# Seven-product matrix schemes: running sums kept in one PSUM bank with ScalarE copies, in place of VectorE additions, and a new written order

## The chip, the cores and the metric

One core of one Trainium2 chip runs the whole program. The metric is device time in microseconds (us). All data is float32.

## The reference, cut to what matters

128 graphs of 64 nodes with 512 features pass through four graph layers, each with a layer norm and a relu ahead of it and a residual around it.

```python
for layer in (L0, L1, L2, L3):                      # x: [128, 64, 512], adj: [128, 64, 64]
    h = maximum(layernorm(x), 0)
    x = x + layer(h, adj)

L0: H = adj != 0
    conv(v, W) = Dn * (H @ (Be * (H.T @ (v @ W.T))))      # Dn, Be: inverse degrees
    h1 = layernorm(relu(conv(h, W1) + b1)) * gamma + beta # 512 -> 1024
    out = conv(h1, W2) + b2 + h                           # 1024 -> 512
L1: s = h @ w @ a;  A = exp(leaky(8 * tanh((s_i + s_j) / 8))) * adj
    out = (A / rowsum(A) * rowsum(adj)) @ h @ w
L2: P = adj * exp((h Wq + bq) (h Wk + bk).T);  out = (P / rowsum(P)) @ (h Wv + bv)
L3: Tr = rownorm(adj * exp(leaky(sj + si + ab)))
    out = relu(h Wk0 + Tr h Wk1 + Tr Tr h Wk2 + biases)
```

## The kernel before, in words

**Tiling.** The 8192 rows are cut into 16 groups of 512 rows, a group being four tiles of 128 rows (two graphs each). Layers 0 and 1 of all 16 groups come first; their results go to memory (`xm`), and layers 2 and 3 of all groups follow.

**The scheme.** Every large weight product is done on 2x2 blocks with seven products in place of eight (a Strassen-Winograd scheme; `strassen`, L589, and `seven`, L568). Of two row tiles and a weight in four blocks it makes sums of blocks (L599 on VectorE, the weights' sums once at the start, L393 to L396), seven products on TensorE (L607, in layer 2 L845), and four results that are sums of products. The products 1, 6 and 7 are running sums: M1, M1+M6 and M1+M6+M7. Layer 0 runs the scheme twice for each half of a group (a product is two matmuls of 512 columns for W1, four of 256 for W2), layer 1 once (two of 256), layer 2 twice for a group (queries and values, four of 256 side by side in one bank), layer 3 once for a half (six of 256). In all there are 64 schemes that fill a bank of 512 columns and 96 that fill 256.

**Sums before.** Each of the products 1, 6, 7 and 5 has a PSUM bank of its own. ScalarE copies M1 to the buffer U (L575), VectorE adds the second (L577) and the third (L579), reading each from PSUM. The products 2, 3 and 4 accumulate in the banks of 1, 5 and 7. The results go out through an emit function: for each of the four, VectorE reads the bank and adds bias, scale or residual; for three of them another operation first adds the running sum (VectorE L625 in W1 of layer 0, GpSimd L635, L799, L865, L899, L987 elsewhere), and the result (0,0) has none.

**What sets the order.** The kernel writes down the order of all instructions itself. Each operation is recorded with an engine, a cost in us and a priority; `Graph.run` (L82) takes for each engine the operation that can start first by these costs, and among equals the one of lowest priority. Priorities come from the group (`PERIOD1`, `PERIOD2`), a stretch for each layer and a shift for each part of the program (`AT`, L281). Buffers are handed out in the same pass; U has two places for 512 columns and one for 256, the transient buffer `qT` two, PSUM eight banks. Where TensorE would stand idle over 0.5 us by these costs, filling matmuls of 128x128 on ones are put in (L1013). At run time nothing is rearranged: each engine takes its list in order, and waits on semaphores.

**Other steps named below.** L467 multiplies Wq by Wk once, from loads L327. L437 needs all of W2. L546 mixes rows by the graph matrix and ScalarE L548 copies the result. L555 and L557 are ScalarE copies of 1024 half-words around a DMA transpose, whose buffer `tmp` is shared with loads of weights that VectorE's L381 consumes. L705 is the first product with the graph matrix. L667, L948, L957 and L973 belong to layer 3's transition matrix and its use; L878 are the logits of layer 2 and L911 its weighted values.

```python
        mul[1](p1, True)
        act(n / 1200 + 0.17, lambda: nc.scalar.copy(at(0)(), p1.t[:, :n]), [p1], [(U, 0)])
        mul[6](p2, True)
        dve(c_v(n), lambda: nc.vector.tensor_add(at(1)(), p2.t[:, :n], at(0)()), [p2, (U, 0)], [(U, 1)])
        mul[7](p4, True)
        dve(c_v(n), lambda: nc.vector.tensor_add(at(2)(), p4.t[:, :n], at(1)()), [p4, (U, 1)], [(U, 2)])
```

Of the kernel before, what the change touches and what calls it, by code (L numbers as in the profile page):

```python
# [11 lines left out]
ALU = mybir.AluOpType  # L12
# [4 lines left out]
D = 512  # L17
# [150 lines left out]
def tile_adj_preln_d4(  # L168
# [6 lines left out]
    nc = tc.nc  # L175
# [37 lines left out]
    for two in TWO:  # L213
        both = work.tile([P, max(sum(size(shape) * n for _, shape, n in tags) for tags in two)], F32,
                         name="_".join(tag for tags in two for tag, _, _ in tags))
        for tags in two:
            at = 0
            for tag, shape, n in tags:
                for i in range(n):
                    v = both[:, at:at + size(shape)]  # L220
# [28 lines left out]


    def c_mm(n, count):
        return 2 * count * max(n * 2 / 2400 + 0.0025, 0.111)

    TR = 0.109

    def c_v(n, from_psum=False):
        return n / 960 + 0.155 + 0.05 * from_psum
# [4 lines left out]
    def dve(cost, fn, r, w):  # L262
        return G.op("DVE", cost, fn, r, w)

    def act(cost, fn, r, w):
        return G.op("ACT", cost, fn, r, w)
# [7 lines left out]
    def quad(b):  # L274
# [2 lines left out]
    FILL = 0.75  # L277


    STRETCH, PERIOD1, PERIOD2 = (2.11, 6.43, 4.5, 0.21), 79.8, 140.53  # L280
    AT = {  # L281
        "x0": -1458.56, "apart": 58.27, "w1": -1207.06, "b1": -1268.61, "w2": 312.2, "w": -214.25, "c1": 103.95,
        "l0": -1592.46, "c2": -560.69, "l1": 125.29, "c": 849.04, "g0": -1279.86, "g1": -1456.39, "g2": -589.08,
        "g3": -1259.16, "g": -1258.76, "bq": 321.93, "l3": 56.2, "wg": 1603.23, "w3": 387.13, "beg0": -72.8,
        "beg1": 73.58, "end00": 0.51, "end01": 19.09, "end11": -75.14, "new2": 31.64, "new3": 4.77, "end2": -39.58,
        "end3": -21.31, "load1": -108.19, "load2": 27.97, "m": 12.29, "h0": 9.53, "p0": 10.98, "z0": -29.14,
        "q0": 15.48, "y0": -518.61, "h1": -26.33, "p1": -22.59, "z1": -30.25, "q1": 4.48, "y1": -2.94, "s": -20.64,
        "t0": -25.67, "e0": -522.9, "t1": -42.32, "e1": -53.88, "hT": 8.77, "sh": 220.05, "lq": 8.14, "pt": -124.53,
        "v": 35.92, "pv": -915.5, "s3": 19.84, "tt": -865.12, "a0": 46.62, "b0": -371.48, "a1": 104.26, "b1_": 198.72,
    }  # L290

    def part(name):
# [272 lines left out]
                nc.tensor.matmul(p.t, lhsT(c), rhs(c), start=first and c == 0, stop=last and c == k - 1)  # L565
        pe(c_mm(512, k), mm, r if first else [*r, p], [p])

    def seven(mul, U, n, emit):  # L568

        p1, p2, p3, p4 = (Buf("ps") for _ in range(4))
        at = lambda i: (lambda: U.t[:, i, :n])
        mul[1](p1, True)
        act(n / 1200 + 0.17, lambda: nc.scalar.copy(at(0)(), p1.t[:, :n]), [p1], [(U, 0)])  # L575
        mul[6](p2, True)
        dve(c_v(n), lambda: nc.vector.tensor_add(at(1)(), p2.t[:, :n], at(0)()), [p2, (U, 0)], [(U, 1)])  # L577
        mul[7](p4, True)
        dve(c_v(n), lambda: nc.vector.tensor_add(at(2)(), p4.t[:, :n], at(1)()), [p4, (U, 1)], [(U, 2)])  # L579
        mul[2](p1, False)  # L580
        emit(0, 0, p1, None, (U, 0))
        mul[5](p3, True)
        emit(1, 1, p3, (U, 2), (U, 2))
        mul[4](p4, False)
        emit(1, 0, p4, (U, 1), (U, 0))
        mul[3](p3, False)
        emit(0, 1, p3, (U, 1), (U, 1))

    def strassen(A, keys, B, kc, n, stag, emit):  # L589

# [30 lines left out]
    def scaled(dst, wdst, scale, ks, add, ka, p, u, v, n):  # L621

        if u is not None:
            (U, i), j, add0 = u, v[1], add
            dve(c_v(n) + 0.2, lambda: nc.vector.scalar_tensor_tensor(U.t[:, j], U.t[:, i], scale(), add0(), op0=ALU.mult, op1=ALU.add), [u, *ks, *ka], [v])  # L625
            add, ka = (lambda: U.t[:, j]), [v]
        dve(c_v(n, True), lambda: nc.vector.scalar_tensor_tensor(dst(), p.t[:, :n], scale(), add(), op0=ALU.mult, op1=ALU.add), [p, *ks, *ka], [wdst])  # L627

    def biased(dst, j, p, u, v, row, krow):

        cols = slice(j * D // 2, (j + 1) * D // 2)
        add, ka = (lambda: row()[:, cols]), krow
        if u is not None:
            (U, iu), iv = u, v[1]
            pool(0.75, lambda: nc.gpsimd.tensor_add(U.t[:, iv], U.t[:, iu], row()[:, cols]), [u, krow], [v])  # L635
            add, ka = (lambda: U.t[:, iv]), v
        dve(c_v(D // 2, True), lambda: nc.vector.tensor_add(dst.t[:, cols], p.t[:, :D // 2], add()), [p, ka], [(dst, j)])

    def across(col, r):

# [122 lines left out]
    def layer1(g):  # L763
        ad = adjs[g]
        sg = Buf("col")
        part("s")

        stats = [pre_stats(g, t) for t in range(T)]
        for t in range(T):
            h = pre_ln(g, t, stats[t])  # L770
            dot(lambda h=h: h.t, lambda: wa_b.t, lambda t=t: sg.t[:, t:t + 1], [h, wa_b], [(sg, t)])
        z = bcast_sum(lambda: sg.t, lambda: sg.t, [(sg, t) for t in range(T)])
        act(0.42, lambda: nc.scalar.activation(z.t, z.t, AF.Tanh, scale=0.125), [z], [z])
        lrelu(z, 0.1)
        act(0.42, lambda: nc.scalar.activation(z.t, z.t, AF.Exp, scale=8.0), [z], [z])


        PT, zz, den, num = Buf("bd"), Buf("ee"), Buf("col"), Buf("col")
        dve(0.42, lambda: nc.vector.tensor_reduce(num.t, ad.t[:, 0], AX.X, ALU.add), [ad], [num])
        dve(0.42, lambda: nc.vector.tensor_mul(zz.t, z.t, ad.t[:, 0]), [z, ad], [zz])  # L780
        dve(0.42, lambda: nc.vector.tensor_reduce(den.t, zz.t, AX.X, ALU.add), [zz], [den])
        dve(0.16, lambda: nc.vector.reciprocal(den.t, den.t), [den], [den])
        dve(0.16, lambda: nc.vector.tensor_mul(den.t, den.t, num.t), [den, num], [den])
        rn = across(lambda: den.t, [den])
        dve(0.42, lambda: nc.vector.tensor_mul(z.t, z.t, ad.t[:, 1]), [ad, zz], [z])
        for s in HALVES:
            dve(0.61, lambda s=s: nc.vector.tensor_mul(PT.t[s, :, s], z.t[s], by_node(rn, s)), [z, rn], [(PT, s.start)])
        PTk = [(PT, 0), (PT, C)]
        step(1.0)
        for t0 in (0, 2):  # L790
            part(f"t{t0 // 2}")
            ph = [left_mul_T(pre_ln(g, t, stats[t]), lambda t=t: PT.t[:, t, :], PTk, "mT") for t in (t0, t0 + 1)]
            step(1.8)

            def emit_w(i, j, p, u, v, t0=t0):
                xx, cols = xt[g, t0 + i], slice(j * D // 2, (j + 1) * D // 2)
                if u is not None:
                    U, iu = u
                    pool(0.75, lambda: nc.gpsimd.tensor_add(xx.t[:, cols], xx.t[:, cols], U.t[:, iu]), [xx, u], [xx])  # L799
                dve(c_v(D // 2), lambda: nc.vector.tensor_add(xx.t[:, cols], p.t[:, :D // 2], xx.t[:, cols]), [p, xx], [xx])  # L800

            part(f"e{t0 // 2}")
            strassen(lambda i, j, ph=ph: ph[i].t[:, 2 * j:2 * j + 2, :], {(i, j): [ph[i]] for i in range(2) for j in range(2)},
                     W, 2, D // 2, "s1", emit_w)
            for t in (t0, t0 + 1):
                xx = xt[g, t]
                xmid[g, t] = dram.tile([P, D], F32, name=f"xm{g}_{t}")
                dma(256, lambda xx=xx, t=t: nc.sync.dma_start(xmid[g, t], xx.t), [xx], [("xmid", g, t)])

    def layer2(g):  # L810
# [44 lines left out]
        def emit_q(i, j, p, u, v):  # L855
            if u is None:
                q = Buf("qT")
                for o in range(2):
                    act(0.38, lambda o=o: nc.scalar.activation(q.t[:, o, :], pair(p.t)[:, o, :], AF.Identity, bias=gb_c[:, 2 * i + o:2 * i + o + 1]), [p, "gb"], [(q, o)])
                qs.append((i, j, lambda: q.t, [(q, 0), (q, 1)]))  # L860
            else:

                (U, iu), iv = u, v[1]
                at = lambda: pair(U.t[:, iv])
                pool(1.3, lambda: nc.gpsimd.tensor_add(at(), pair(U.t[:, iu]), gb_c[:, 2 * i:2 * i + 2, None].to_broadcast([P, 2, 2 * P])), [u, "gb"], [v])  # L865
                dve(c_v(D), lambda: nc.vector.tensor_add(at(), pair(p.t), at()), [p], [v])
                qs.append((i, j, at, [v]))

        seven({n: prod(WG[n], hs[n], True) for n in range(1, 8)}, Buf("u5"), D, emit_q)


        def logits():
# [20 lines left out]
        def emit_v(i, j, p, u, v):  # L893
# [3 lines left out]
            if u is not None:  # L897
                (U, iu), iv = u, v[1]
                pool(1.3, lambda: nc.gpsimd.tensor_add(pair(U.t[:, iv]), pair(U.t[:, iu]), bias), [u, "bv_b"], [v])  # L899
                add, ka = (lambda: pair(U.t[:, iv])), v  # L900
            dve(c_v(D), lambda: nc.vector.tensor_add(vb[i].t[:, :, at], pair(p.t), add()), [p, ka], [(vb[i], j)])


        hv = {**hs, 3: hs[4], 4: hs[3], 5: hs[7], 7: hs[5]}
# [16 lines left out]
    def layer3(g):  # L921
# [39 lines left out]
        for t0 in (0, 2):  # L961
# [21 lines left out]
            def emit_o(i, j, p, u, v, t0=t0):  # L983
# [4 lines left out]
                    add2, ka = (lambda: U.t[:, iv]), v  # L988
                else:
                    add2 = add  # L990
                dve(c_v(D // 2), lambda: nc.vector.tensor_add(U.t[:, iv], p.t[:, :D // 2], add2()), [p, ka], [v])
                dve(c_v(D // 2), lambda: nc.vector.scalar_tensor_tensor(xx.t[:, cols], U.t[:, iv], 0.0, xx.t[:, cols], op0=ALU.max, op1=ALU.add), [v, xx], [(xx, j)])
                if (i, j) in ((1, 0), (0, 1)):
                    r = (g * T + t0 + i) * P
# [135 lines left out]
```

## Time and profile before

| | |
|---|---|
| median of 3 runs | 2374.13 us (2373.94 to 2375.01) |
| the profiled execution, first to last instruction | 2373.3 us, 0.8 us under the median of the runs |
| TensorE (PE) busy | 2349.7 us, 99% |
| VectorE (DVE) busy | 1742.1 us, 73% |
| ScalarE (ACT) busy | 1268.7 us, 53% |
| GpSimd (POOL) busy | 958.7 us, 40% |
| TensorE passes | 12008 (a float32 matmul is two passes) |

PE counts overlapping passes, so its busy share says little of how much of the time is needed work; the distance between the starts of passes says more. The program has 6004 matmuls, 82 of them filling ones. Layers 0 and 1 last until about 1170 us, layers 2 and 3 from about 1310 us; between them the two overlap.

### The profile page before, as it was taken

What the parts mean: (1) busy time and instruction counts of PE and PEld (TensorE: products, weight loads), DVE (VectorE), ACT (ScalarE), POOL (GpSimd) and SP (SyncE); (2) the same over time, 40 slices, a digit from 0 to 9 for tenths busy, and PEclk for the clock granted to TensorE, in tenths of its full rate; (3) what the DMA queues carried; (4) which work ended last, traced back from release to release, by engine and by line L of the source; (5) the groups of instructions that cost most, each with busy time, mean ns of one, the idle gap of its engine ahead of it and who ended that gap; (6) DMA issues with size and microseconds to landing.
All of it is one profiled execution on the core that took longest, in us unless ns stands there. A gap on an engine that the chain in (4) does not pass through costs nothing.

```text
span 2373.3 us, 33860 instructions
## 1 busy us (share of the span) xinstructions
PE 2349.7 (99%) x12008; PEld 1867.5 (79%) x12008; DVE 1742.1 (73%) x3798; ACT 1268.7 (53%) x1746; POOL 958.7 (40%) x1514
## 2 busy tenths in 40 slices
PE   9999999999999999999999999999999999999999
PEld 4677677777677776677788888888888888888887
DVE  7888778788778788777868566666666766667764
ACT  4566656567565576565745445444445444454422
POOL 6244455544455444555443323333323333323330
PEclk9999999999999999999999999999999999999999
DMA  7333222333223333232532322213322223322211
GB/s 258 80 80 65 54 68 64 71 80 63 50 68 69 72 80 54 55 73 71 133 106 59 76 69 61 69 45 69 76 64 65 64 52 73 71 63 65 48 36 40
DMA packets 336922, 171.02 MB, mean 72 GB/s; under 512 B 284656, under 2 KB 290672, under 8 KB 336752
## 3 DMA queue, kind: packets, MB, share of 16 engines
q1 hardware_dynamic: 336752, 168.86, 29.5%
q8 instruction: 94, 1.54, 0.3%
q14 instruction: 76, 0.62, 0.1%
HBM read 66.99 MB, written 34.70 MB: 43 GB/s over the span
## 4 chain that ended last, share of the span: by engine, by line
PE 89%; DVE 5%; DMA 3%; ACT 1%; issue 1%; POOL 1%; SPq 1%; DVEq 0%; ACTq 0%
PE ps L607 61%; PE ps L845 14%; PE ps L546 4%; PE ps L911 2%; PE ps L758 2%; PE ps L973 2%; PE ps L878 1%; DMA x<-xm 1%; DVE st L516 1%; PE ps L957 0%; DMA rw<-row 0%; PE ps L705 0%; DVE tmp_mB_s L599 0%; DVE o L381 0%; PE ps L467 0%
## 5 line engine op out<-in xcount | busy, mean ns | idle before, releaser
L537 ACT ACTIVATE h<-x,nm,rs 128x512 f32<-128x512 f32 x384 | 300.2, 810 | 399.6 <-POOL nm L524 366.8
L607 PE MATMUL ps<-wb_mem,s_s_a 128*128 128x256 f32 x2184 | 512.0, 380 | 0.3
L607 PEld LDWEIGHTS ps<-wb_mem,s_s_a 128*128 128x128 f32 x2184 | 409.5, 190 | 74.0 <-issue 19.8
L518 POOL TENSOR_SCALAR rs<-mv 128x1 f32<-128x1 f32 x320 | 99.2, 310 | 493.0 <-DVE mv L517 477.5
L607 PE MATMUL ps<-wb_mem,tmp_mB_s 128*128 128x256 f32 x1152 | 262.4, 380 | 3.2 <-DVE tmp_mB_s L599 3.1
L607 PEld LDWEIGHTS ps<-wb_mem,tmp_mB_s 128*128 128x128 f32 x1152 | 218.1, 190 | 35.3 <-DVE tmp_mB_s L599 5.4
L607 PE MATMUL ps<-wb_mem,mT_a 128*128 128x256 f32 x1016 | 242.0, 380 | 0.0
L607 PE MATMUL ps<-wa_mem,mT_a 128*128 128x512 f32 x512 | 237.3, 595 | 3.9 <-ACT mT_a L548 3.9
L607 PE MATMUL ps<-wb_mem,rT_vu_tt 128*128 128x256 f32 x1024 | 238.2, 380 | 0.6 <-ACT rT_vu_tt L557 0.6
L607 PEld LDWEIGHTS ps<-wb_mem,rT_vu_tt 128*128 128x128 f32 x1024 | 192.8, 191 | 41.3 <-issue 12.5
L607 PEld LDWEIGHTS ps<-wb_mem,mT_a 128*128 128x128 f32 x1016 | 192.2, 190 | 31.8 <-issue 5.7
L516 DVE BATCH_NORM_STATS2 st<-x 128x6 f32<-128x512 f32 x256 | 173.6, 678 | 45.8 <-DMA x<-xm 40.6
L519 POOL TENSOR_TENSOR rs<-rs,mhalf 128x1 f32<-128x1 f32 x320 | 193.3, 604 | 26.4
L607 PEld LDWEIGHTS ps<-wa_mem,mT_a 128*128 128x128 f32 x512 | 97.1, 190 | 112.7 <-issue 102.4
L607 PE MATMUL ps<-wa_mem,s_s_a 128*128 128x512 f32 x384 | 180.7, 593 | 0.3 <-DVE z_hT L627 0.3
L987 POOL TENSOR_TENSOR u<-u,bk_b 128x256 f32<-128x256 f32 x96 | 76.4, 796 | 238.9 <-DVE u L579 170.2
L575 ACT COPY u<-ps 128x256 f32<-128x256 f32 (+1 forms) x160 | 72.7, 454 | 177.8 <-PE ps L845 105.1
L635 POOL TENSOR_TENSOR u<-u,row_sh 128x256 f32<-128x256 f32 x96 | 74.9, 789 | 228.1 <-DVE u L577 211.6
L733 ACT ACTIVATE z_hT<-z_hT 128x512 f32<-128x512 f32 x128 | 79.6, 627 | 157.8 <-DVE z_hT L627 157.8
L557 ACT COPY rT_vu_tt<-z_hT 128x1024 uint16<-128x1024 uint16 x128 | 147.1, 1159 | 13.7 <-DMA z_hT<-tmp_mB_s 13.3
L546 PEld LDWEIGHTS ps<-bd,h 128*128 128x128 f32 x1024 | 131.1, 192 | 26.6 <-issue 22.2
L524 POOL TENSOR_SCALAR nm<-mv,rs 128x1 f32<-128x1 f32 x320 | 138.5, 433 | 31.1
(174 smaller groups left out, 4336.0 us busy)
## 6 DMA issues: line engine op xcount, KB each, us to landing
x<-in_x_dram SPq DMA_DIRECT2D x64, 256.0 KB, 2.7
xm<-x SPq DMA_DIRECT2D x64, 256.0 KB, 2.1
x<-xm SPq DMA_DIRECT2D x64, 256.0 KB, 2.8
out_dram<-x SPq DMA_DIRECT2D x64, 256.0 KB, 2.0
adj<-in_adj_dram SPq DMA_DIRECT2D x32, 256.0 KB, 4.0
rw<-row SPq DMA_DIRECT2D x94, 64.0 KB, 2.8
wb_mem<-in_Wk_dram SPq DMA_DIRECT2D x6, 512.0 KB, 5.3
tmp_mB_s<-in_Wk_dram SPq DMA_DIRECT2D x8, 256.0 KB, 3.1
```

Source lines behind the costliest of these rows:

```text
L516: dve(0.69, lambda i=i: nc.vector.bn_stats(st.t[:, i, :], src(i)), [r[i]], [(st, i)])
L518: pool(0.32, lambda: nc.gpsimd.tensor_scalar_add(rs.t, mv.t[:, 1:2], EPS), [mv], [rs])
L519: pool(0.65, lambda: nc.gpsimd.tensor_tensor(rs.t, rs.t, mhalf, ALU.pow), [rs], [rs])
L524: pool(0.47, lambda: nc.gpsimd.tensor_scalar(nm.t, mv.t[:, 0:1], rs.t, -1.0, op0=ALU.mult, op1=ALU.mult), [mv, rs], [nm])
L537: act(0.82, lambda: nc.scalar.activation(h.t, xx.t, AF.Relu, bias=nm.t, scale=rs.t), [xx, nm, rs], [h])
L546: nc.tensor.matmul(quad(p)[:, c, :], h.t[:, c * P:(c + 1) * P], rhs(), start=True, stop=True)
L557: act(1.16, lambda: nc.scalar.copy(u16(dst()).rearrange("p c (k q) -> p c k q", q=2), u16(back()).rearrange("p (q c r) -> p c r q", q=2, c ...
L607: nc.tensor.matmul(p.t[:, :n], lhs()[:, c, :], rhs(c), start=first and c == 0, stop=c == kc - 1, skip_group_check=True)
L635: pool(0.75, lambda: nc.gpsimd.tensor_add(U.t[:, iv], U.t[:, iu], row()[:, cols]), [u, krow], [v])
L733: act(0.63, lambda: nc.scalar.activation(z.t[:, cols], z.t[:, cols], AF.Relu), [(z, j)], [(z, j)])
L845: nc.tensor.matmul(pair(p.t)[:, o, :], a, b, start=first and o == 0 and c == 0, stop=c == 1, skip_group_check=True)
L987: pool(0.88, lambda: nc.gpsimd.tensor_add(U.t[:, iv], U.t[:, u[1]], add()), [u, ka], [v])
```

## The change

`seven` uses three banks. Product 6 and then product 7 are accumulated onto product 1 in the same bank; ScalarE copies the bank to U after each (`snap`). Product 4 is accumulated last in that bank, and its result is read from the bank with no further sum. Product 2 has a bank of its own and takes M1 from U. Product 5 is copied by ScalarE as well (to U, or to a `qT` buffer for the queries of layer 2), so that product 3 can be accumulated onto it; the result (1,1) is made of the two copies. The order of the products is 1, 2, 6, 5, 7, 3, 4 in place of 1, 6, 7, 2, 5, 4, 3. The emit functions read either a bank or a copy (`pv`).

The planner's cost of a matmul changes, and so do all stretches, periods and shifts, and by them the order of every engine's list. The list has 89 filling matmuls: 13 among the first 80 rows of TensorE's list, 44 where the layers overlap, 30 in fifteen pairs spread over layers 2 and 3, and 2 near the end. The loads of Wq and Wk stand first in the list of DMAs, ahead of adj and x.

```diff
     def c_mm(n, count):
-        return 2 * count * max(n * 2 / 2400 + 0.0025, 0.111)
+        return 2 * count * max(n * 2 / 2400 + 0.0045, 0.1115)
...
-    STRETCH, PERIOD1, PERIOD2 = (2.11, 6.43, 4.5, 0.21), 79.8, 140.53
+    STRETCH, PERIOD1, PERIOD2 = (2.2224, 5.134, 0.2702, 0.07), 81.1, 134.563
     AT = {
-        "x0": -1458.56, "apart": 58.27, "w1": -1207.06, "b1": -1268.61, "w2": 312.2, "w": -214.25, "c1": 103.95,
...
+        "x0": -2840.94, "apart": 287.74, "w1": -513.31, "b1": -168.3, "w2": 243.98, "w": 957.54, "c1": 854.05, "l0":
...
-    def seven(mul, U, n, emit):
-        p1, p2, p3, p4 = (Buf("ps") for _ in range(4))
-        at = lambda i: (lambda: U.t[:, i, :n])
-        mul[1](p1, True)
-        act(n / 1200 + 0.17, lambda: nc.scalar.copy(at(0)(), p1.t[:, :n]), [p1], [(U, 0)])
-        mul[6](p2, True)
-        dve(c_v(n), lambda: nc.vector.tensor_add(at(1)(), p2.t[:, :n], at(0)()), [p2, (U, 0)], [(U, 1)])
-        mul[7](p4, True)
-        dve(c_v(n), lambda: nc.vector.tensor_add(at(2)(), p4.t[:, :n], at(1)()), [p4, (U, 1)], [(U, 2)])
-        mul[2](p1, False)
-        emit(0, 0, p1, None, (U, 0))
-        mul[5](p3, True)
-        emit(1, 1, p3, (U, 2), (U, 2))
-        mul[4](p4, False)
-        emit(1, 0, p4, (U, 1), (U, 0))
-        mul[3](p3, False)
-        emit(0, 1, p3, (U, 1), (U, 1))
+    def pv(p):
+        t = p[0].t[:, p[1]] if isinstance(p, tuple) else p.t
+        return t.rearrange("p a b -> p (a b)") if len(t.shape) == 3 else t
+
+    def seven(mul, U, n, emit, fifth=None):
+        px, py, pz = (Buf("ps") for _ in range(3))
+        fifth = fifth or (U, 0)
+
+        def snap(p, v):
+            act(n / 1200 + 0.17, lambda: nc.scalar.copy(pv(v)[:, :n], p.t[:, :n]), [p], [v])
+
+        mul[1](px, True)
+        snap(px, (U, 0))
+        mul[2](py, True)
+        emit(0, 0, py, (U, 0), (U, 0))
+        mul[6](px, False)
+        snap(px, (U, 1))
+        mul[5](pz, True)
+        snap(pz, fifth)
+        mul[7](px, False)
+        snap(px, (U, 2))
+        emit(1, 1, fifth, (U, 2), (U, 2))
+        mul[3](pz, False)
+        emit(0, 1, pz, (U, 1), (U, 1))
+        mul[4](px, False)
+        emit(1, 0, px, None, (U, 0))
...
-        seven({n: prod(WG[n], hs[n], True) for n in range(1, 8)}, Buf("u5"), D, emit_q)
+        seven({n: prod(WG[n], hs[n], True) for n in range(1, 8)}, Buf("u5"), D, emit_q, Buf("qT"))
```

## The prediction

> **What bounds the kernel now.** I read the page's shares first, then the table by stage, then the timeline around each place where TensorE stood.
>
> ```profile
> PE 2349.7 (99%) x12008; PEld 1867.5 (79%) x12008; DVE 1742.1 (73%) x3798; ACT 1268.7 (53%) x1746; POOL 958.7 (40%) x1514
> ```
>
> ```profile
> 0.00:100.00 100.00, 91.89 (x309) 51.67 (x310) 80.53 (x159) 46.25 (x68) 47.74 (x70) 0.97 0.63 194
> 100.00:1170.00 1070.00, 1068.87 (x4531) 776.54 (x4530) 857.16 (x1887) 674.72 (x932) 520.35 (x824) 1.00 0.30 69
> 1170.00:1310.00 140.00, 135.52 (x817) 117.76 (x816) 108.93 (x238) 69.59 (x95) 55.08 (x90) 0.99 0.37 91
> 1310.00:2317.00 1007.00, 1002.56 (x6063) 876.67 (x6061) 672.92 (x1469) 468.21 (x637) 330.98 (x524) 1.00 0.26 62
> 2317.00:2373.00 56.00, 50.84 (x296) 44.82 (x294) 22.54 (x48) 9.95 (x16) 4.57 (x7) 0.96 0.14 41
> ```
>
> The first is the page's line of shares. In the second view the columns are the stretch, its length, then busy time and count for PE, weight loads, DVE, ACT and POOL, then granted clock, DMA share and GB/s. TensorE is the bound in every stretch. DVE is 80% busy in the first two, ACT 63% in the second.
>
> Busy time counts overlapping passes, so I also summed distances between starts. Undisturbed, a pass of 256 columns starts 0.216 us after the last, one of 512 columns 0.429, one of 128 columns 0.112 (0.056 at L973), one of L878 0.033. With the program's counts, 7424 x 0.216 + 1080 x 0.429 + 1024 x 0.112 + 1024 x 0.056 + 1024 x 0.033 + 268 short ones x 0.11 = about 2302 us are needed passes, which the change leaves alone. The 82 filling matmuls take 82 x 0.224 = 18.4. The rest of 2373.3 is 52.8: 1.0 before the first pass, 4.0 after the last, and between passes, by the same sum for each stage, 14.8, 2.4, 9.0, 17.2 and 3.5. Nothing else is there to win: some 65 us.
>
> ```profile
> 70.53 3.24 PE L607 MATMUL ps<-wa_mem,mT_a 128*128 128x512 f32 x4 [3.89 <-ACT mT_a L548]
> ...
> 2320.45 3.96 PE L1013 MATMUL ps<-ones 128*128 128x128 f32 x34
> 2325.85 1.10 PE L957 MATMUL ps<-rT_vu_tt,bd 128*128 128x64 f32 x8 [1.44 <-DVE rT_vu_tt L948]
> 2326.79 0.66 PE L1013 MATMUL ps<-ones 128*128 128x128 f32 x4
> 2327.42 5.41 PE L973 MATMUL ps<-rT_vu_tt,h 64*128 64x128 f32 x64
> ```
>
> Two examples (start, length, what, and in brackets idle time and releaser). At 66.6 TensorE stops 3.9 us for a ScalarE copy. Behind it ScalarE waited 5.2 us with a copy L555 for a `tmp` buffer that VectorE had not yet read, VectorE being busy without a break with weight sums and L381. Near the end only filling matmuls stand between layer 3's last chain and its use; 64 passes then take 5.4 us where 64 x 0.056 = 3.6 are due.
>
> **What the Trainium skill says.** "TensorE: Matmul & The Clock Gate", Part 1: after an idle window of about 3.4 us the array runs at half clock, until it has been busy for another. The trace agrees: the clock is 0.5 for 3.4 us at 71 and at 2327 us, each costing 1.7 us more. "PSUM — Partial Sum Buffer", PSUM bank collisions: TensorE and a reader must not be in one bank at once, so product 6 waits for the copy of M1 to end; no lag on top is stated. The trace has 0.2 us from the last pass's successor to a ScalarE copy (PE at 1413.24, ACT at 1413.44), and 0.05 us from a copy's end to the waiting pass (below). The same page, Engine vs sequencer instructions: ScalarE, VectorE and GpSimd take their lists strictly in order, so a copy behind a waiting one waits too; the 5.2 us above show it. Prices are the trace's.
>
> **The change, part by part.**
>
> ```profile
> L577 DVE TENSOR_TENSOR u<-ps,u 128x512 f32<-128x512 f32 x64 | 43.5, 680 | 12.1 <-PE ps L607 6.2 <-PE ps L845 5.9
> L575 ACT COPY u<-ps 128x512 f32<-128x512 f32 x64 | 37.4, 584 | 113.9 <-PE ps L845 105.1 <-PE ps L607 8.8
> L575 ACT COPY u<-ps 128x256 f32<-128x256 f32 x96 | 35.3, 368 | 63.8 <-PE ps L607 44.6 <-issue 13.2 <-DVE mv L517 3.6
> ```
>
> *Engine work.* VectorE loses L577 and L579: 64 x (0.680 + 0.686) + 96 x (0.422 + 0.421) = 168 us, from 73% to 66%. ScalarE goes from one copy for each scheme to four: 192 x 0.584 + 288 x 0.368 = 218 us more, from 53% to 63%; between 100 and 1170 us, with 32 schemes of 512 and 64 of 256, 127 us more, from 63% to 75%. Neither becomes the bound. The emit work keeps its count; (1,1) is now read from SBUF, which costs VectorE 0.793 (L625, all SBUF) against 0.746 (L627, PSUM), so under 64 x 0.05 = 3 us off the path. Matmuls: seven more fills.
>
> *New waits.* Each of products 6, 7, 4 waits for a ScalarE copy of the bank that it writes, product 3 for the copy of product 5; queued behind on PE is everything. In the written order I took, for each scheme product, the TensorE work between the bank's last use and the next. Under 1 us it is 51 times (before 16), from 1.5 to 2 us 128 times (before 36). A copy of 256 columns needs 0.2 + 0.37 + 0.05 = 0.62 against 0.86 in the narrowest (layer 1), one of 512 needs 0.2 + 0.58 + 0.05 = 0.83 against 1.73. So they fit as long as ScalarE is free; in layer 1's narrow run its list has the copies next to each other. What happens when not:
>
> ```profile
> 1237.41 1.04 ACT L555 COPY o<-h 128x1024 uint16<-128x1024 uint16 x1
> 1238.36 0.57 ACT L575 COPY u<-ps 128x512 f32<-128x512 f32 x1
> ...
> 1238.98 1.99 PE L845 MATMUL ps<-z_hT,wa_mem 128*128 128x256 f32 x8 [0.32 <-ACT u L575]
> ```
>
> Here a copy stood behind L555, and the next product, 1.73 us later in the bank, came 0.48 us late by starts. Also, the copy of product 5 goes where M1 was: ScalarE waits for the emit of (0,0) to have read it, mostly on GpSimd (0.8 us), which has two products' time.
>
> *100 to 1170 us.* Before, 2.4 us are lost. Of 52 tight reuses before one was late, so of 179 some four will be, 2 us in all; I put the 2 here (bounds 0 and 8, a third of the 51 narrow ones late by 0.48).
>
> *Start.* By hand with the trace's DMA landings (one of 256 KB each 0.7 us): Wq and Wk first brings L467 from 10.1 to about 4.3 us, at half clock for a part of it; adj and x come about 1 us later, hidden behind those 16 matmuls. The first two W1 products and all of L467 end near 27.7 us, where before the same work ends at 30.6: -2.9 (bounds -4 and +1). L437 is then reached early, and the last load of W2, behind a weight load that needs a `tmp` buffer, lands near 40: +2.2 (0 to +4). Nine fills after that become two: 7 x 0.224 = -1.6. The stop at 66.6 costs 4.0 and 1.7 for the clock; five schemes by then relieve VectorE of up to 10 x 0.68 = 7 us, but I take only 3.5 of the 5.7, since ScalarE's list grows there. Sum -5.8 (-11 to +3).
>
> *Where the layers overlap.* 44 fills for 43, other work alone on PE: +0.2 (-5 to +5).
>
> *1310 to 2317 us.* The 30 fills cost 30 x 0.224 = +6.7: they are placed where the planner sees TensorE idle, before product 6 and the logits. Of the 17.2 lost, 10.1 lie before L607 and L911, that is behind VectorE's block sums and layer 2's emits (waits named: `tmp_mB_s` L599 and `ve` L914); VectorE drops by 71 us there, and I take half, -5. Late copies beyond those above +1. Sum +2.7 (-8 to +12).
>
> *End.* L667 is now followed by three products and so is L957, 6 x 2 x 0.216 x 3 = 7.8 us, where the chain from L667 to L957 took 8.0. 17 fills fewer are -3.8; of the 3.5 lost I leave 0.7, with no idle window and so no half clock. Sum -6.6 (-7.7 to 0). The last product's emit stays two VectorE steps and a store.
>
> Together 2.0 - 5.8 + 0.2 + 2.7 - 6.6 = -7.5, so 2365.8 in the profiled execution, and 2366.6 beside the median.
>
> **The rivals.**
>
> *The relief goes further* (2356): the stop at 66.6 goes whole, and VectorE's 10.1 us in layers 2 and 3 as well: start -8.5, then -3.4, end -6.6. For it: DVE is the busiest after PE. Against: many waits there are for chains, not for load.
>
> *Nothing changes* (2374): the ends win 12, and the fills with new ScalarE waits in the middle give it back. The list has those 30 fills; that is a plan for idle time where before there was none.
>
> *Slower* (2384): the running bank becomes a chain through ScalarE. The place is the 128 + 51 tight reuses, 127 more than before, most in layers 1 and 2; the price is one copy of 1.04 to 1.16 us ahead in ScalarE's list, 0.48 us as seen. L555 and L557 fill (134 + 132 + 147 + 73 + 50 + 24) / 2373 = 24% of ScalarE's time; if ScalarE's fuller list puts one ahead of every second tight copy, 90 x 0.48 = 43 us, and with 12 won at start and end and the fills in layers 2 and 3 covering some 20 of it, about +10. It decides from about 25 late ones, 12 us. Against it: of the 52 tight reuses before, matched to their passes, one alone was late.
>
> **How the numbers follow.** The forecast has 0.43 (its own range 2360 to 2373), the further relief 0.12, no change 0.20, slower 0.25. About 0.2% (4.7 us) is what a measurement of this kernel can tell from no change. Faster by over that is below 2369.4: 0.7 of the forecast and the first rival, 0.42; within it the rest of the forecast and nearly all of "nothing changes", 0.31; slower 0.27. The range from 2353 to 2386 takes in the rivals' values, and leaves out a larger relief and a larger chain.
>
> **What would show it.** Right: no wait over 2 us on PE between 50 and 100 us; L973 at the end near 3.6 us for 64 passes, and no fills of 17; DVE near 1575 and ACT near 1487 us busy; 100 to 1170 us losing under 5 us. Wrong: PE waiting for ScalarE's `u` copies by over 10 us in all, a half clock in layers 2 and 3, or a new stop before L437.

## The result, and the profile after

The changed kernel takes 2403.5 us (median, 2403.1 to 2406.2), the kernel before 2374.6 us beside it on the same chip (2373.9 to 2375.0). The ratio is 1.0123, with an interval from 1.0109 to 1.0137: slower by 29 us, where 7.5 us less were forecast. The profiled execution spans 2400.9 us, 27.6 more than that of before.

First the page's line of shares, then the table by stage (stretch, its length, busy time and count of PE, weight loads, DVE, ACT and POOL, granted clock, DMA share, GB/s). The border before the last stretch stands 28 us later than in the table of before, so that the last stretch holds about the same work.

```profile
PE 2357.4 (98%) x12022; PEld 1866.8 (78%) x12022; DVE 1636.8 (68%) x3478; ACT 1454.4 (61%) x2226; POOL 976.9 (41%) x1514
```

```profile
0.00:100.00 100.00, 90.19 (x283) 48.10 (x284) 81.64 (x147) 52.95 (x82) 50.12 (x66) 0.95 0.63 195
100.00:1170.00 1070.00, 1054.07 (x4424) 759.55 (x4423) 798.62 (x1669) 755.31 (x1169) 514.01 (x814) 1.00 0.29 65
1170.00:1310.00 140.00, 134.75 (x838) 116.80 (x838) 104.02 (x223) 86.11 (x132) 64.96 (x97) 1.00 0.39 103
1310.00:2345.00 1035.00, 1026.29 (x6193) 896.66 (x6192) 631.54 (x1402) 548.39 (x823) 341.98 (x530) 1.00 0.27 63
2345.00:2400.90 55.90, 52.07 (x291) 45.69 (x289) 21.01 (x40) 11.67 (x23) 5.79 (x8) 1.00 0.13 38
```

The work did move as planned: VectorE is down by 105 us and ScalarE up by 186. But in the second row TensorE gets through 107 passes fewer than before in the same 1070 us, at full clock. VectorE is 75% busy there and ScalarE 71%, so TensorE is not short of work because one of them is full: something makes it wait. I took the prediction's own sum for each stage again (time between starts of passes beyond their undisturbed spacing), with the filling matmuls, counted by the time at which they run, beside it at 0.224 us each:

| stage | lost before | lost after | fills | change | predicted |
|---|---|---|---|---|---|
| start, to 100 us | 14.8 | 18.8 | 17 to 11 | +2.7 | -5.8 |
| 100 to 1170 | 2.4 | 22.3 | 7 to 2 | +18.7 | +2.0 |
| overlap | 9.0 | 8.8 | 39 to 48 | +1.8 | +0.2 |
| 1310 to the end's chain | 17.2 | 23.0 | 0 to 28 | +12.1 | +2.7 |
| end | 3.5 | 0.4 | 19 to 0 | -7.4 | -6.6 |

The sum is +27.9, against 27.6 between the spans. Two thirds of it lie in layers 0 and 1. The list of TensorE's waits (waiting line, releaser, us in total, times, longest; waits under 0.15 us are not listed) names where:

```profile
PE ps L769 <- DVE y_qT L648: 12.9, 12, 1.6
PE ps L618 <- ACT u L582: 7.4, 16, 3.1
PE ps L922 <- DVE rT_vu_tt L912: 4.2, 8, 0.6
PE ps L968 <- DVE rT_vu_tt L959: 3.4, 7, 1.0
```

The second line is the rival chain through ScalarE, and it is the smaller one: 9.4 us in all with 2.0 at L856, of which 3.1 are one stop near the start. Counted by starts of passes, with the short waits, it is some 13 us. The first line is new. L769 is the last step of layer 0 (L758 before), which multiplies the graph matrix by y; L648 is the emit that writes y. Following it back in the timeline of one group (start, length, what, idle time and releaser):

```profile
435.34 0.39 SPq L339 DMA_DIRECT2D adj<-in_adj_dram  x1
...
437.32 0.21 DVE L518 BATCH_NORM_AGGREGATE mv<-st 128x2 f32<-128x12 f32 x1
...
439.78 0.42 DVE L790 TENSOR_REDUCE col<-adj 128x4 f32<-128x256 f32 x1 [2.25 <-DMA adj<-in_adj_dram]
440.12 0.42 DVE L648 TENSOR_TENSOR y_qT<-u 128x256 f32<-128x256 f32 x1
...
440.45 0.42 DVE L648 TENSOR_TENSOR y_qT<-ps,u 128x256 f32<-128x256 f32 x1
...
440.92 1.13 PE L769 MATMUL ps<-y_qT,bd 128*128 128x512 f32 x2 [1.12 <-DVE y_qT L648]
```

VectorE is free at 437.5 and stands 2.25 us with a row sum of the next group's adj (L790, needed only in layer 1), because the load that was issued at 435.34 lands 4.4 us later. The y emits are next in its list, and TensorE waits 1.12 us behind them. Over the whole program this row sum waits 33.3 us in 14 groups:

```profile
L790 DVE TENSOR_REDUCE col<-adj x16: 386/420/421, 6.4 to 1028.5; 128x4 f32<-128x256 f32 x16
its engine sat idle before it (us, times) until:
  DMA adj<-in_adj_dram: 33.3, 14
```

Before, the same instruction (L779) began 9 to 24 us after the issue, mostly 22, and the same view names no wait. The row sum reads adj alone, nothing of the seven products. It is the new written order that put it there.

**Theories.** Theory 1: most of the loss is the order, that is, the place of instructions in the engines' lists, first of all this row sum. Theory 2, the rival: TensorE is held by ScalarE's copies between products in one bank, and the row sum is beside the point.

### The profile page after: what moved, and what is told of

It is laid out like the page before. It is cut to its first block, busy times and chain, and to the rows that moved or that the text cites. A ratio compares the mean times of both kernels' runs of the same rounds, so it can differ in the third digit from the quotient of the medians.

```text
span 2400.9 us, 33897 instructions
## 1 busy us (share of the span) xinstructions
PE 2357.4 (98%) x12022; PEld 1866.8 (78%) x12022; DVE 1636.8 (68%) x3478; ACT 1454.4 (61%) x2226; POOL 976.9 (41%) x1514
## 4 chain that ended last, share of the span: by engine, by line
PE 76%; DVE 10%; DMA 6%; POOL 4%; ACT 2%; issue 1%; SPq 0%; DVEq 0%; ACTq 0%; POOLq 0%
PE ps L618 56%; PE ps L856 8%; PE ps L547 4%; DMA adj<-in_adj_dram 2%; PE ps L769 2%; PE ps L984 2%; PE ps L922 1%; DMA rw<-row 1%; POOL nm L525 1%; POOL rs L520 1%; POOL x L810 1%; DVE st L517 1%; DMA row<-col 1%; DVE x L928 1%; DVE rT_vu_tt L959 1%
## 5 line engine op out<-in xcount | busy, mean ns | idle before, releaser
L582 ACT COPY u<-ps 128x256 f32<-128x256 f32 (+1 forms) x624 | 274.7, 452 | 450.6 <-PE ps L618 279.0
L618 PE MATMUL ps<-wb_mem,s_s_a 128*128 128x256 f32 x2184 | 507.2, 380 | 3.4 <-ACT u L582 3.4
L618 PEld LDWEIGHTS ps<-wb_mem,s_s_a 128*128 128x128 f32 x2184 | 410.8, 190 | 68.2 <-issue 8.5
L519 POOL TENSOR_SCALAR rs<-mv 128x1 f32<-128x1 f32 x320 | 108.5, 339 | 458.6 <-DVE mv L518 443.4
L618 PE MATMUL ps<-wb_mem,tmp_mB_s 128*128 128x256 f32 x1152 | 259.8, 380 | 0.7 <-ACT u L582 0.7
L618 PE MATMUL ps<-wa_mem,mT_a 128*128 128x512 f32 x512 | 241.7, 600 | 3.3 <-ACT u L582 3.3
L618 PEld LDWEIGHTS ps<-wb_mem,tmp_mB_s 128*128 128x128 f32 x1152 | 218.1, 190 | 30.9 <-ACT u L582 1.5
L618 PE MATMUL ps<-wb_mem,rT_vu_tt 128*128 128x256 f32 x1024 | 241.2, 379 | 0.5 <-ACT rT_vu_tt L558 0.5
L618 PE MATMUL ps<-wb_mem,mT_a 128*128 128x256 f32 x1016 | 237.8, 379 | 0.0
L618 PEld LDWEIGHTS ps<-wb_mem,rT_vu_tt 128*128 128x128 f32 x1024 | 192.6, 190 | 53.1 <-issue 28.4
L520 POOL TENSOR_TENSOR rs<-rs,mhalf 128x1 f32<-128x1 f32 x320 | 209.4, 655 | 25.2
L618 PEld LDWEIGHTS ps<-wb_mem,mT_a 128*128 128x128 f32 x1016 | 192.3, 190 | 31.8 <-issue 6.2
L618 PE MATMUL ps<-wa_mem,s_s_a 128*128 128x512 f32 x384 | 178.2, 594 | 0.0
L618 PEld LDWEIGHTS ps<-wa_mem,mT_a 128*128 128x128 f32 x512 | 96.4, 192 | 100.9 <-issue 92.3
L525 POOL TENSOR_SCALAR nm<-mv,rs 128x1 f32<-128x1 f32 x320 | 146.3, 457 | 31.5
L547 PEld LDWEIGHTS ps<-bd,h 128*128 128x128 f32 x1024 | 131.7, 193 | 31.3 <-issue 13.2
L810 POOL TENSOR_TENSOR x<-x,u 128x256 f32<-128x256 f32 x96 | 76.7, 799 | 166.5 <-ACT u L582 166.5
L556 ACT COPY tmp_mB_s<-z_hT 128x1024 uint16<-128x1024 uint16 x128 | 133.7, 1045 | 10.1 <-DVE o L382 5.6
```

What stands on the lines that cost most here:

```text
L519: pool(0.32, lambda: nc.gpsimd.tensor_scalar_add(rs.t, mv.t[:, 1:2], EPS), [mv], [rs])
L520: pool(0.65, lambda: nc.gpsimd.tensor_tensor(rs.t, rs.t, mhalf, ALU.pow), [rs], [rs])
L525: pool(0.47, lambda: nc.gpsimd.tensor_scalar(nm.t, mv.t[:, 0:1], rs.t, -1.0, op0=ALU.mult, op1=ALU.mult), [mv, rs], [nm])
L547: nc.tensor.matmul(quad(p)[:, c, :], h.t[:, c * P:(c + 1) * P], rhs(), start=True, stop=True)
L556: act(1.05, lambda: nc.scalar.copy(u16(planes.t).rearrange("p (q c) -> p q c", q=2), u16(src()).rearrange("p (c q) -> p q c", q=2)), ksrc, ...
L582: act(n / 1200 + 0.17, lambda: nc.scalar.copy(pv(v)[:, :n], p.t[:, :n]), [p], [v])
```

## Experiments

**The row sum alone, moved late in the changed kernel.** All lists stay as they were, save that each L790 stands right ahead of the one instruction that uses it.

```diff
+        early = {o.tag[1]: (t, q, o) for t, q, o in order if o.tag and o.tag[0] == "num"}
+        order = [e for _, q, o in order if not (o.tag and o.tag[0] == "num")
+                 for e in ([early[o.tag[1]]] if o.tag else []) + [(_, q, o)]]
```

> The changed kernel, with one instruction for each group of layer 1 moved in VectorE's list: the row sum of the next adj (L790) stands right ahead of its only use, no longer ahead of the y emits (L648). All else of the order is as in the changed kernel. Theory 1 (the written order: this row sum waits for adj's load 33 us in all, the y emits behind it, and TensorE's L769 behind them): the 14.8 us that TensorE loses between L618 and L769 from 100 to 1170 us go nearly all, so 2388 to 2391 us, a gain of 12 to 15 us, and L769 waits under 3 us for y. Theory 2 (TensorE waits for ScalarE's copies between products in one bank): the row sum is not on the path, 2403 us within 2.

Measured 2385.0 us, 1.0052 of before (1.0035 to 1.0068) against 1.0123. By the ratios that is 17 us less, by the spans 18.6, and so somewhat more than the 12 to 15 expected. The loss from 100 to 1170 us falls from 22.3 to 6.6. In the list of waits for this kernel L773 is the old L769, and the lines above it are other steps:

```profile
PE ps L622 <- ACT u L586: 6.0, 17, 1.7
PE ps L926 <- DVE rT_vu_tt L916: 3.9, 8, 0.6
...
PE ps L773 <- DVE y_qT L652: 0.6, 1, 0.6
```

So one instruction of 0.42 us for each group, in the wrong place of a list, is some 60% of the loss (67% by the spans).

**The reverse: the row sum early in the kernel before.**

```diff
...
+        from_ = sorted((t + 2.7, o.tag[1]) for t, q, o in order if o.tag and o.tag[0] == "adj")
+        order = [e for e in order if not (e[2].tag and e[2].tag[0] == "num")]
+        order = sorted(order + [(t, -1, early[g][2]) for t, g in from_], key=lambda x: x[:2])
```

> The kernel before, with the row sum of each next adj (L779) moved forward in VectorE's list to about 2 us after adj's load was issued, so ahead of three of the four y emits, as the changed order has it; its result goes to a buffer of its own, and the seven products are those of before. Theory 1: VectorE waits some 2 us for adj in each group, TensorE loses about 1.2 us in each of 13 or so groups: 10 to 16 us more than before, 2384 to 2390 us. Theory 2: the place of this one instruction does not matter, 2374 us within 2.

Measured 2380.0 us, 1.0032 (1.0019 to 1.0045), 7.5 us more. The sign is right, the size was too high: in that list VectorE comes to the row sum later after the issue, so it waits 11.3 us in 14 groups and not 33, and the loss from 100 to 1170 us rises by 5.9. The old scheme pays for such a place as well.

**The planner's number behind it.** The planner lets a load of 256 KB land 2.7 us after its issue begins. In the trace of the changed kernel the loads of x, of that size, do so (2.7 us, median), but those of adj take 4.1. The kernel before was planned with the same 2.7; its numbers only happened to put the row sum later. Here only adj's landing is changed, and all is planned anew.

```diff
-        dma(256, lambda: nc.sync.dma_start(b.t, adj[g]), [], [b])
+        dma(256, lambda: nc.sync.dma_start(b.t, adj[g]), [], [b]).late = 1.8
...
-            end = t + o.cost + self.LATENCY[o.eng]
+            end = t + o.cost + self.LATENCY[o.eng] + o.late
```

> The changed kernel with one number of the planner put right: a load of adj lands 4.5 us after its issue begins, as the trace has it, where the planner reckoned 2.7. The whole order is planned anew by this; it has 103 filling matmuls for 89, which is 3 us more. Theory 1 (the loss from 100 to 1170 us is this one wrong landing time): VectorE waits for adj by under 10 us in all where it waited 33, the 15 us at L769 go, and with the fills 2388 to 2394 us. If the loss came from the scheme or the other numbers: 2403 to 2408 us.

Measured 2388.7 us, 1.0070 (1.0055 to 1.0085): some 13 us less than the change, with 14 fills more. The row sum's waits for adj fall by two thirds (to 11.7 us, where under 10 were expected), and the loss from 100 to 1170 us to 7.7:

```profile
L791 DVE TENSOR_REDUCE col<-adj x16: 366/420/422, 5.5 to 1015.7; 128x4 f32<-128x256 f32 x16
its engine sat idle before it (us, times) until:
  DMA adj<-in_adj_dram: 11.7, 13
```

**What the copies cost.** The order of the changed kernel, but ScalarE's copies move 32 columns (182 ns each in place of 371 and 581), except in layer 2's queries; the rest of those sums is left out of the results.

```diff
-            act(n / 1200 + 0.17, lambda: nc.scalar.copy(pv(v)[:, :n], p.t[:, :n]), [p], [v])
+            act(n / 1200 + 0.17, lambda: nc.scalar.copy(pv(v)[:, :m], p.t[:, :m]), [p], [v])
```

> The changed kernel at its own order, but ScalarE's copies of the running sums move 32 columns in place of 256 or 512, except in the queries of layer 2. The other columns of those sums are left out of the results; all else runs as before. It takes some 70% of the duration off 600 copies and so bounds what copies cost in time. Theory 2 (the chain through ScalarE is the loss): 15 to 28 us less, 2375 to 2388 us. Theory 1 (the order is the loss, the copies fit beside other work): under 5 us less, 2398 to 2403 us; TensorE's waits for copies were 9 us in all in the profile of the changed kernel, of which a part goes.

Measured 2394.0 us, 1.0090 (1.0075 to 1.0105), 8 us less. That is below what theory 2 asked for and above what I had given theory 1: copies of 32 columns win some 8 of the 29 us, with L769 still losing 12.0 us between passes. By stages the loss between passes falls by 1.4 us at the start, 5.0 from 100 to 1170 and 4.4 after 1310 us, and rises by 1.6 where the layers overlap. Not all of the 5.0 is the copies' doing: in the run without late fills (below), whose lists up to there are those of the changed kernel, L769 loses 12.2 us and the stage 2.9 less than in the changed kernel. So something that runs through the copies does cost time, but how much of it falls in this stage one trace can't say. The next two runs look for it.

**A shared place behind them.** With the row sum late, 4.2 us remained at the first product after a mixing, 0.38 us in each of 12 groups. The timeline of that kernel at one of them:

```profile
385.84 1.17 POOL L814 TENSOR_TENSOR x<-x,u 128x256 f32<-128x256 f32 x1
...
386.97 1.26 POOL L737 TENSOR_TENSOR x<-x,h 128x512 f32<-128x512 f32 x1
387.04 1.47 DVE L815 TENSOR_TENSOR x<-u,x 128x256 f32<-128x256 f32 x1 [0.62 <-POOL x L814]
...
388.55 0.37 ACT L586 COPY u<-ps 128x256 f32<-128x256 f32 x1 [1.81 <-DVE x L815]
...
388.97 0.91 PE L622 MATMUL ps<-wb_mem,s_s_a 128*128 128x256 f32 x3 [0.22 <-ACT u L586]
```

The result (1,1) is now read from U. Its add (L815) waits for GpSimd's L814, then lasts 1.47 us where 0.41 is usual, beside GpSimd's L737; the copy of the next scheme's M1 goes to the same place of U (there is one for 256 columns) and waits 1.81 us; product 6 accumulates in the bank being copied, and waits for that. The edit gives product 5's copy a buffer of its own:

```diff
-        fifth = fifth or (U, 0)
+        fifth = fifth or (Fifth if n == D // 2 else tuple)((U, 0))
...
-        t = p[0].t[:, p[1]] if isinstance(p, tuple) else p.t
+        t = fifth_t if isinstance(p, Fifth) else p[0].t[:, p[1]] if isinstance(p, tuple) else p.t
```

> The kernel with the late row sum (2385 us), and the copy of product 5 in the schemes of 256 columns goes to a buffer of its own, no longer to the place of M1; the order of all lists is the same. In the run before this one TensorE still lost 0.38 us in each of 12 groups at the first product after a mixing (4.2 us in all): ScalarE's copy of the next M1 waits there for VectorE to read product 5's copy from the same place. Theory 1 (the order, and beside it this shared place): these 4.2 us go, 2380 to 2382 us. Theory 2 (copies are late because ScalarE is full): the place does not matter, 2385 us within 2.

Measured 2382.0 us, 1.0042 (1.0028 to 1.0055). In the trace the stage loses 3.0 us where it lost 6.6, near the 4.2 expected; in the whole only 1.5 us (spans) to 2.9 us (medians) come out, which the intervals don't tell from none. The other stages lose about 2 us more. So from 100 to 1170 us the new scheme in the mended order loses as little as the old one (2.4).

**Short copies in the mended order.** The same cut to 32 columns as above, with the same columns left out.

> The kernel with the late row sum and product 5's copy apart (2382 us), with ScalarE's copies of the running sums cut to 32 columns, except in the queries of layer 2; the other columns are left out of the results. It asks how much of the 9 us that short copies won in the changed kernel was the same time as the two mends won. If copies as such still hold TensorE up: 9 us less again, 2373 us. If, as theory 1 has it, part of those 9 us was the stall at the shared place and the queue around the row sum: 4 to 5 us less, 2377 to 2378 us, most of it from 1310 us on.

Measured 2379.7 us, 1.0036 (1.0022 to 1.0051): 1.4 us less by the ratios, 3.7 by the spans, 2.9 of it from 1310 us on. Below both expectations by the ratios. From 100 to 1170 us short copies win nothing more (3.1 us lost for 3.0), so what they won there the two mends had won by then. With the fills in place and the queries' copies whole, the length of the copies costs TensorE some 1 to 4 us of 2400; the intervals of the two runs overlap.

**The fills in layers 2 and 3.**

```diff
-        for _ in range(int(gap * FILL / (0.224 if filled else 0.448))):
+        for _ in range(0 if 12 <= len(filled) < 27 else int(gap * FILL / (0.224 if filled else 0.448))):
```

> The changed kernel without the fifteen pairs of filling matmuls that are spread over layers 2 and 3. If they stand on the path for nothing, each costs its 0.224 us: 6.7 us less, 2396.7 us. If they only take up time in which TensorE would have waited anyway, no change, 2403 us within 1.5, and 6.7 us more of waits between passes from 1310 to 2317 us.

Measured 2400.6 us, 1.0120 (1.0105 to 1.0135): 0.7 us less by the ratios, which is no difference, and 3.9 less by the spans. The loss between passes in that stage rises by 4.2 us where 6.7 of fills went. So the fills mostly cover real waits, as their placing said; my +6.7 for them was rightly on the bill, but as waits. And they are mostly the waits of theory 2: the rise is at L856 (7.0 to 11.4 us between passes from 1310 us on), and over the whole program its passes that start late behind a copy to `u` go from 4, costing 2.6 us, to 14, costing 6.0. In every second group, where a pair of fills stood ahead of product 6 of the queries, product 7 now starts some 0.3 us late behind ScalarE's copy. Most of these waits are too short for the list, which has 2.0 us in 3 for the changed kernel and here:

```profile
PE ps L856 <- ACT u L582: 3.0, 5, 1.3
```

So in layer 2 the new scheme pays for its copies in part with fills. Both runs with short copies kept these fills and the full copies of the queries, so they don't see this part.

**Either half alone.** The old seven products with the new numbers, and the new ones with the old numbers.

> One half of the change alone: the seven products of the kernel before, with the changed costs, periods and shifts of the planner. The list has 369 filling matmuls for 82, 64 us more of them. If the numbers alone were the loss of 29 us and the scheme free, about 2403 us plus what of the 64 us is not cover: 2410 to 2470. If the scheme were the loss, it would stay near 2374 plus the same.

> The other half alone: the new seven products with the planner's numbers of the kernel before. The list has 551 filling matmuls, 105 us more than before, ten of them in each group of layer 0, where the planner sees the next scheme wait. The row sum of adj stands early here too. If numbers and scheme only fit each other, it is the slowest of the four, 2440 to 2500 us; if the changed numbers were the loss by themselves, it would be under 2400.

Measured 2465.1 us (1.0387, 1.0372 to 1.0403) and 2546.9 us (1.0732, 1.0714 to 1.0750). The first lies in the range for the numbers alone, which its fills make wide. It has 287 fills more, 64 us, and 28 us beyond them (22 by the spans); from 100 to 1170 us it loses 21.8 us with the old scheme, as much as the changed kernel, though mostly at L547 waiting for `bd`, and its row sum waits only 3 times. The second is 47 us above my range: 105 us of fills and 69 beyond, among them 22 us at L967, behind VectorE's transposes L958, and some 14 at L983. Numbers and scheme belong together, so this pair can't divide the loss between them; the edits at a fixed order do.

**All mends together.** Late row sum, product 5's copy apart, no fills in layers 2 and 3, and at the start two `tmp` copies behind the copies that TensorE waits for:

```diff
+        for k, n in ((0, 1), (1, 2)):
+            i = [i for i, (_, _, o) in enumerate(order) if o.tag == ("plane",)][k]
+            j = [j for j, (_, _, o) in enumerate(order) if j > i and o.eng == "ACT"][n - 1]
...
+            order[j:j] = move
```

> The kernel with the late row sum and product 5's copy apart, and two more edits of the order: the fifteen pairs of filling matmuls in layers 2 and 3 are left out (3 us by the run without them), and in the first 70 us two of ScalarE's copies ahead of a DMA transpose, each waiting for a tmp buffer, stand behind the one and the two copies that TensorE waits for. Theory 1: 2380 to 2382 less 3 for the fills and less 2 to 4 for the start, 2373 to 2377 us, so level with the kernel before. Theory 2 (a full ScalarE): 2380 us or more.

Measured 2379.6 us, 1.0032 (1.0021 to 1.0044). That is still slower than before, misses the 2373 to 2377 expected, and can't be told from the run without the last two edits (1.0028 to 1.0055). By the number alone it lies at the mark set for theory 2. By stages it loses 2.8 us from 100 to 1170 us, so there theory 1 holds; from 1310 us on it loses 26.9 where 17.2 were lost before, and 10.5 us of the whole are late starts behind copies to `u`, so there part of the rest is theory 2. The edit at the start failed: the stop only moved on, to L468 (L451 in the changed kernel), which waits 6.4 us in two stops for VectorE's L466.

## Why the prediction was wrong, step by step

**100 to 1170 us: the step that failed, +2 against +18.7.** "Before, 2.4 us are lost. Of 52 tight reuses before one was late, so of 179 some four will be, 2 us in all." I looked at the new order only for bank reuse, the thing that the scheme changes. The order of the other lists was new as well, and I did not compare VectorE's instructions that depend on a load with the place of that load in SP's list. Before, adj landed 4.0 us after its issue; in the new list VectorE is free for the row sum about 2 us after it, ahead of the y emits. Both were there to be read. In place of the 2 us for late copies came 14.8 us at L769, behind the row sum's 33.3 us of waiting; with the row sum moved the stage loses 6.6. The term for bank reuse itself was too small, but inside its bounds of 0 to 8: TensorE's listed waits for copies are 2.5 us in this stage and 4.3 by starts, and none of the 4.3 is left once product 5's copy has its own buffer. The prediction saw that shared place in one direction only: product 5's copy waiting until M1 is read, not the next M1 waiting until product 5's copy is read.

**Start: +2.7 against -5.8.** The stop at 66.6 us was to lose more than half of its 5.7. The timeline of the changed kernel there:

```profile
64.67 0.69 DVE L382 SCALAR_TENSOR_TENSOR o<-tmp_mB_s 128x512 f32<-128x512 f32 x1 [0.97 <-DMA tmp_mB_s<-in_Wv_dram]
...
65.45 1.04 ACT L556 COPY tmp_mB_s<-z_hT 128x1024 uint16<-128x1024 uint16 x1 [5.58 <-DVE o L382]
...
66.40 0.85 ACT L582 COPY u<-ps 128x512 f32<-128x512 f32 x2
...
67.03 3.78 PE L618 MATMUL ps<-wa_mem,mT_a 128*128 128x512 f32 x4 [3.08 <-ACT u L582]
```

It is the same stop: the `tmp` copy waits 5.6 us for the same work of VectorE, and the copies that TensorE needs stand behind it. VectorE in its turn waits 0.97 us here for a load of weights into such a buffer; how much of the 5.6 is VectorE's load and how much the buffers was not separated. The stop costs 3.1 us, and the four passes after it run at half clock (3.78 us), so about 5 where 5.7 were lost before and 2.2 forecast. The failed term is the 3.5 us of relief: VectorE's lighter load did not end this wait sooner. Other stops came in: by starts 1.9 us at L443, 1.4 at L618, 1.2 at L451 and 1.9 at L547. L468 (L467 before) does begin at 4.28 us, as forecast, but the first mixing then waits, so the first W1 products and all of L468 end at 30.0 us and not at 27.7.

**1310 to 2317 us: +12.1 against +2.7.** The fills came as priced (28 of them here, 6.3 us). The half of 10.1 us that I gave to VectorE's relief came at one place and was lost at others: the loss at L607 did shrink (5.9 to 1.9), but the new order has layer 3's chain and layer 2's values late on VectorE (L968, behind L959: 4.6 us; L922, mostly behind L912: 7.5 for 4.2). Neither goes away with the row sum or without the fills. Short copies take 3 us off L968 and none off L922. Which placing would cure them was not tried, so their cause stays open.

**Where the layers overlap: +1.8 against +0.2.** Right within its bounds. **End: -7.4 against -6.6.** Right, and for the reason given: no fills stand there, and 64 passes take 3.8 us at full clock.

```profile
2348.02 1.00 PE L968 MATMUL ps<-rT_vu_tt,bd 128*128 128x64 f32 x8
2348.86 2.81 PE L618 MATMUL ps<-wb_mem,mT_a 128*128 128x256 f32 x12
...
2356.78 3.84 PE L984 MATMUL ps<-rT_vu_tt,h 64*128 64x128 f32 x64
```

**Engine work.** ScalarE came to 1454 us (1487 expected), VectorE to 1637 (1574 expected). Some 25 of VectorE's 63 us too many are the result (1,1), "under 3 us off the path": the prediction priced it for the 64 schemes of 512 columns from an operation that read SBUF alone, and the time went into the adds of 256 columns, see below. Some 28 more are older operations with inputs in SBUF alone (L610, L382, L636), which last longer in the new order; why was not looked into. Of the rivals, the slower one had the sign right, but mainly by another mechanism: late copies cost some 13 us by starts and part of what the fills cover, not 43.

## What to carry to other kernels

When an edit comes with a new written order, the order can be the larger part of the change, as here: compare every engine's list, and for each instruction that waits for a load, the time from the issue to the place where it stands against the landing time that the trace shows. In an engine that takes its list in order, a 0.4 us instruction that nobody needs yet can hold whatever is behind it. And work taken off an engine is worth something only where that work ends a wait: VectorE was busy for 105 us less, and of the waits forecast to shrink by it only that at L607 did so clearly, by 4 us.

## What the runs showed of the hardware that was not expected

A VectorE addition with both operands in SBUF can take over three times as long when it begins beside a long GpSimd operation; one with an operand in PSUM does not. The groups of the changed kernel (mean in ns after the busy us), the new form of (1,1) beside the old one:

```profile
L648 DVE TENSOR_TENSOR y_qT<-u 128x256 f32<-128x256 f32 x32 | 27.1, 848 | 25.4 <-POOL u L646 25.4
L648 DVE TENSOR_TENSOR y_qT<-ps,u 128x256 f32<-128x256 f32 x64 | 26.2, 409 | 6.9 <-PE ps L618 5.7 <-POOL u L646 1.2
...
L811 DVE TENSOR_TENSOR x<-u,x 128x256 f32<-128x256 f32 x32 | 24.9, 778 | 8.1 <-POOL x L810 8.0
```

Of the 64 adds of the new form, 40 take 0.39 to 0.43 us and 24 take 1.47 to 1.49. The Trainium skill, "SBUF — State Buffer", "SBUF: two separate sides", says why this can be: VectorE with two SBUF inputs and a GpSimd operation that reads SBUF take one shared pair of ports as a lock for the whole instruction. The trace agrees: each of the 24 began 0.07 to 0.08 us after the start of a GpSimd addition of 128x512 (always L733, which is L737 in the timeline above and reads SBUF), and ended 0.28 us after its end, to a hundredth. Of the 40 others six began during a GpSimd operation, each on a single column. In the same two lines 20 adds with an operand in PSUM began during a GpSimd operation of 256 or 512 columns, and took 0.43 us at most. In all this is 32 x (0.848 - 0.409) + 32 x (0.778 - 0.419) = 25.5 us more on VectorE. That the lock and nothing else makes these long was not tried by an edit.
